# A CIN kernel on one core: first transfers, first gathers and first products in another order

## Chip, cores and metric

The kernel runs on one core of a Trainium2 chip. The metric is the device time of one execution, in microseconds (us). Before the change the median of 7 runs is 767.29 us, from 765.71 to 769.38.

## What is computed

Three layers of a compressed interaction network on `x` of shape (1024, 39, 64), then a linear layer. Cut to what matters:

```python
def _cin_layer(Xk, X0, W, b):
    Wr = W.reshape(O, Hk, Fdim)
    return jnp.einsum('bhe,bfe,ohf->boe', Xk, X0, Wr) + b[None, :, None]
X0 = sparse_embedding; Xk = X0; outs = []
for W, b in ((W0, b0), (W1, b1), (W2, b2)):
    Xk = _cin_layer(Xk, X0, W, b)
    outs.append(Xk.sum(axis=-1))
y = jnp.concatenate(outs, axis=-1) @ fc_w.T + fc_b
```

Nothing but sums follows the second and third layer, so the kernel folds their weights with `fc_w` ahead of the main loop. What is left per batch block are products of pairs of fields, `x[i] * x[k]`, and one matrix multiplication of each with 128 output rows (64 of layer 1, 64 of the folded rest).

## The kernel before, in words

**Blocks and steps.** The batch is cut into 32 blocks of 2048 columns (32 samples by 64). A block needs six "pairs" of tiles (128 x 2048 each), and two neighbouring blocks share one "half" step of 64 + 64 rows: 208 steps in all. In each, VectorE multiplies two SBUF tiles into `p` (line 377, or 379 for the half step `u * v`), and TensorE multiplies `p` with the 128 x 128 weights `wa[:, c]` into PSUM (line 391). The head of the list is `(0,0) (0,1) (0,3) (1,0) (1,1) (1,3) (0,2) (0,4) (0,5) (0,6) (1,2) (1,4) (1,5)`: block, then pair; pair 6 is the half step. I call them step 0 to step 12 and their products p0 to p12. Pairs 0 to 5 take the tiles (0,1), (0,2), (0,3), (1,2), (2,3), (1,3) of the block. There are four `p` buffers, so product k waits for the matmuls of step k-4.

**Tiles.** The four tiles of a block, and `u` and `v`, are gathered row by row from a table in DRAM, `xd` (line 122, indirect DMAs that GpSimd issues, 1 MB each). I write r00 for tile 0 of block 0, r13 for tile 3 of block 1. `xd` is filled from `x` by `load` (line 115; blocks 0 and 1 on GpSimd's queue, later ones on SyncE's) and a row of ones (line 188). The gathers' index lists are worked out by some 45 tiny VectorE operations.

**Weights.** The folded weights go through a DRAM table too. `w2` (lines 182, 190) times `fc` gives V2 (matmuls `pv`, line 278, four transposes, line 289, copies, lines 293 and 294); V2 times `w1` gives `pt` and `pr` (lines 322 and 331); these and `w0` make `part` and `rest`, which three DMAs write into `table` (lines 342 to 344). From there two gathers per pair c, `wa` and `wb` (line 351), fetch the rows of both orders of the fields, and VectorE adds them (line 471, `add(c)`). I write wa0, wb0 for pair 0.

**What sets the order.** All of it is written by hand. Each engine works its own list in the order of the program text. GpSimd's list in the head is: load 0, load 1, r00, r01, r02, r10, r11, then, when `table` has landed, wa0 wb0 wa1 wb1 wa3 wb3 r12 wa2 wb2 r03 wa4 wb4 wa5 wb5 u v wa6 wb6 r13, and then the tiles of block 2. VectorE's list behind p4 is p5 p6 p7 add2 p8 add4 p9 add5 p10 add6 p11. The framework gives each transfer one of eight semaphores in turn, eight for the queues of SyncE and ScalarE together and eight for GpSimd's: the ninth transfer is issued only when the first has landed. So ScalarE's issue of `w0s` (line 196) waits for three earlier transfers, and ScalarE's copies of `fc` (lines 199, 200), which `pv` needs, stand behind it in ScalarE's list. `spin(n)` is n matmuls on zeros that keep TensorE busy while it waits (lines 209 to 211).

## Time and profile before

| what | value |
|---|---|
| profiled execution, device time | 766.58 us |
| its span of instructions | 764.8 us, so 1.8 us lie around it |
| TensorE busy in the span | 743.5 us (97%) |
| VectorE / ScalarE / GpSimd busy | 641.2 (84%) / 160.2 (21%) / 318.8 us (42%) |
| bytes moved by DMA | 181.79 MB, mean 238 GB/s |
| matmuls of the main loop (line 391), 1792 records | 722.5 us busy |

A row of the timeline is: start in us, duration in us, engine, line, operation, output<-input, and in brackets the engine's idle time ahead of it with what ended it. In the chain of waits a row is: start, duration, what. A TensorE step of 128 rows is 4 matmuls of 512 columns in 32-bit floats, which the trace records as 8 passes. A GpSimd row of an indirect DMA is the time in which GpSimd issues it, not the time in which the bytes move.

### The profile page before, as it was taken

The page shows a single profiled execution, that of the slowest core. Times are in us where ns is not written, and L with a number is a line of the kernel's source. Part 1 is how long each engine was busy: PE and PEld are TensorE (multiplying, and loading weights), DVE is VectorE, ACT ScalarE, POOL GpSimd, SP SyncE. Part 2 cuts the span into 40 slices and gives each one's busy share as a digit, 9 for nine tenths or more (in the row PEclk, how much of TensorE's full clock was granted, in tenths as well). Part 3 has the DMA queues.
Part 4 walks back from the last instruction along what each step waited for, and adds up shares of the span by engine and source line. Part 5 has one row for each costly group of instructions (what it writes and reads, how often), then busy time and mean ns, then how long its engine had stood idle before and what let it go on. Part 6 is the DMA issues. An engine that isn't in the chain of part 4 may idle for free.

```text
span 764.8 us, 5146 instructions
## 1 busy us (share of the span) xinstructions
PE 743.5 (97%) x1856; PEld 321.7 (42%) x1856; DVE 641.2 (84%) x479; ACT 160.2 (21%) x207; POOL 318.8 (42%) x185
## 2 busy tenths in 40 slices
PE   6598999999999999999999999999999999999998
PEld 1243444444444444444444444444444444444443
DVE  5375998899888888988888988888988888998885
ACT  2002311112221212222121222112122221112212
POOL 4387173532436354243624425363442636334200
PEclk9899999999999999999999999999999999999999
DMA  8849968575875757686565777657577764738400
GB/s 251 274 169 370 404 192 340 194 270 204 330 250 218 277 171 270 231 327 241 206 279 170 279 248 301 250 186 287 183 288 253 273 263 145 284 150 314 165 0 0
DMA packets 62839, 181.79 MB, mean 238 GB/s; under 512 B 41364, under 2 KB 41499, under 8 KB 42254
## 3 DMA queue, kind: packets, MB, share of 16 engines
q0 software_dynamic: 23712, 169.34, 57.7%
q1 hardware_dynamic: 38494, 11.36, 6.3%
q10 hardware_dynamic: 608, 0.77, 0.4%
q8 instruction: 14, 0.23, 0.1%
q14 instruction: 11, 0.09, 0.0%
HBM read 180.58 MB, written 11.10 MB: 251 GB/s over the span
## 4 chain that ended last, share of the span: by engine, by line
PE 91%; DMA 4%; issue 2%; POOL 1%; DVE 0%; ACT 0%; SPq 0%; DVEq 0%; POOLq 0%
PE po L391 91%; DMA table<-part 1%; DMA wb<-table,wlists 1%; DMA u<-xd,lists 1%; POOL wa L351 1%; DMA b0s<-in_b 1%; POOL wb L351 1%; DMA fc<-in_fc_w 1%; PE pv L278 0%; DMA xd<-in_x 0%; PE pt L322 0%; PE idle L211 0%; POOL r L122 0%; DVE g L430 0%; DVE part L337 0%
## 5 line engine op out<-in xcount | busy, mean ns | idle before, releaser
L391 PE MATMUL po<-p,wa 128*128 128x512 f32 (+1 forms) x1792 | 722.5, 595 | 10.7 <-DVE wa L471 10.6
L377 DVE TENSOR_TENSOR p<-r 128x2048 f32<-128x2048 f32 x192 | 434.3, 2290 | 88.4 <-PE po L391 82.0
L391 PEld LDWEIGHTS po<-p,wa 128*128 128x128 f32 (+1 forms) x1792 | 314.4, 190 | 418.1 <-issue 394.4
L122 POOL DMA_INDIRECT r<-xd,lists x128 | 248.8, 1944 | 365.3 <-DVE p L377 339.0
L410 ACT ACTIVATE x<-po,b0s 64x512 f32<-64x512 f32 x124 | 84.3, 683 | 355.0 <-PE po L391 348.4
L404 ACT COPY g<-u 39x1024 f32<-39x1024 f32 x64 | 66.6, 1043 | 214.8 <-DVE sums L421 176.2
L416 DVE SCALAR_TENSOR_TENSOR g<-po,fc,x 64x512 f32<-64x512 f32 x124 | 86.4, 734 | 0.0
L421 DVE TENSOR_REDUCE sums<-g 103x16 f32<-103x1024 f32 x62 | 75.6, 1220 | 2.1
L379 DVE TENSOR_TENSOR p<-u,v 128x2048 f32<-128x2048 f32 x16 | 36.6, 2285 | 7.6 <-DMA v<-xd,lists 7.6
L122 POOL DMA_INDIRECT u<-xd,lists x16 | 28.6, 1786 | 4.9 <-issue 4.6
L122 POOL DMA_INDIRECT v<-xd,lists x16 | 17.2, 1075 | 4.9 <-issue 4.9
L351 POOL DMA_INDIRECT wa<-table,wlists x7 | 9.3, 1330 | 15.3 <-DMA xd<-in_x 13.4
L211 PE MATMUL idle<-zeros 128*128 128x512 f32 x24 | 12.9, 686 | 1.5 <-DVE fc L171 1.5
L351 POOL DMA_INDIRECT wb<-table,wlists x7 | 10.8, 1544 | 2.1 <-issue 2.1
L471 DVE TENSOR_TENSOR wa<-wa,wb 128x128 f32<-128x128 f32 x7 | 2.1, 300 | 9.9 <-DMA wa<-table,wlists 7.9
L278 PE MATMUL pv<-w2s,fc 64*32 64x320 f32 x16 | 2.8, 765 | 5.8 <-DMA b0s<-in_b 5.8
L211 PEld LDWEIGHTS idle<-zeros 128*128 128x128 f32 x24 | 4.8, 212 | 8.2 <-issue 6.8
L430 DVE SCALAR_TENSOR_TENSOR g<-po,fc,x1q 64x512 f32<-64x512 f32 x4 | 3.0, 743 | 5.3 <-ACT x1q L429 5.3
L289 DVE STREAM_TRANSPOSE blocks<-pv 64x320 f32<-64x320 f32 x4 | 2.1, 513 | 5.0 <-PE pv L278 4.8
L429 ACT ACTIVATE x1q<-po,b0s 64x512 f32<-64x512 f32 x4 | 2.7, 684 | 10.2 <-PE po L391 10.2
L278 PEld LDWEIGHTS pv<-w2s,fc 64*32 64x32 f32 x16 | 1.0, 142 | 8.0 <-issue 7.3
L432 DVE TENSOR_REDUCE sums<-g 103x8 f32<-103x512 f32 x4 | 2.7, 686 | 0.1
(74 smaller groups left out, 30.2 us busy)
## 6 DMA issues: line engine op xcount, KB each, us to landing
xd<-in_x SPq DMA_DIRECT2D x30, 312.0 KB
r<-xd,lists POOLq DMA_INDIRECT x128
w2s<-in_w SPq DMA_DIRECT2D x2, 312.0 KB
xd<-in_x POOLq DMA_DIRECT2D x2, 312.0 KB
w1s<-in_w SPq DMA_DIRECT2D x2, 312.0 KB
table<-part SPq DMA_DIRECT2D x1, 320.0 KB
table<-part ACTq DMA_DIRECT2D x1, 320.0 KB
w0s<-in_w0t ACTq DMA_DIRECT2D x2, 156.0 KB
```

What stands on the lines that cost most here:

```text
L122: nc.gpsimd.indirect_dma_start(dst, None, table, bass.IndirectOffsetOnAxis(ap=lists[:, k : k + 1], axis=0))
L211: nc.tensor.matmul(idle, zeros[:, 0:128], zeros, start=True, stop=True)
L278: nc.tensor.matmul(pv[k][32 * u : 32 * u + 32, 0:320], fc2[rows], w2v[rows, f0 : f0 + 10, :], start=True, stop=True,)
L351: nc.gpsimd.indirect_dma_start(w[:, c], None, table[:], bass.IndirectOffsetOnAxis(ap=wlists[:, k, c : c + 1], axis=0))
L377: nc.vector.tensor_tensor(p, rt[n % 2][:, i], rt[n % 2][:, k], ALU.mult)
L379: nc.vector.tensor_tensor(p, ut[n // 2 % 2], vt[n // 2 % 2], ALU.mult)
L391: nc.tensor.matmul(po[n + h][m], wa[w, c, :], p[w, bass.ts(m, MM)], start=c == opens[n + h], stop=c == closes[n + h],)
L404: nc.scalar.copy(gt[H : H + F], ut[n // 2 % 2][h : h + F, bass.ts(m, SUB)])
L410: nc.scalar.activation(x1[m // 2][:, bass.ts(m % 2, MM)], po[n][m][H:128], AF.Identity, bias=b0s[H:128])
L416: nc.vector.scalar_tensor_tensor(gt[0:H, at], po[n][m][0:H], fc[:, 0:1], x1[m // 2][:, at], ALU.add, ALU.mult)
L421: nc.vector.tensor_reduce(sums[:, b_at : b_at + SB], gt.rearrange("p (b e) -> p b e", e=E), AX.X, ALU.add)
L430: nc.vector.scalar_tensor_tensor(gt[0:H], po[n][m][0:H], fc[:, 0:1], t, ALU.add, ALU.mult)
```

## The change

Four parts, all in the head of the program.

- **First transfers.** `w2` and `w1` are split over SyncE's and ScalarE's queues instead of SyncE's alone; `w0s` and `w0r` go from ScalarE's queue to SyncE's; the two rows of ones for table 0 go from ScalarE's queue to GpSimd's, ahead of load 1. SyncE and ScalarE together then have eight transfers ahead of the biases. The memsets of `v2` and `rest` go from GpSimd to VectorE, and the two copies of `fc` into `fc2` stand ahead of those into `v2`.
- **Gathers.** Only r00 and r01 are issued ahead of the weights' table. GpSimd's list behind it is now: wa0 wb0 r02 wa1 wb1 r10 r11 wa3 wb3 r12 wa2 wb2 r03 u v wa4 wb4 wa5 wb5 wa6 wb6 r13.
- **VectorE.** The list for u and v is worked out behind the V2 copies, the lists for the weights' gathers behind the `part` and `rest` copies. In the main loop's head the order p0 p1 add0 p2 add1 add3 p3 becomes p0 add0 p1 add1 p2 add3 p3.
- **TensorE.** `spin(9)` becomes `spin(11)`.

```diff
         nc.vector.memset(fc2, 0.0)
+        nc.vector.memset(v2, 0.0)
         nc.vector.memset(ones, 1.0)
+        nc.vector.memset(rest[:, NR], 0.0)
         load(0, nc.gpsimd)
         nc.gpsimd.memset(w0s, 0.0)
         nc.gpsimd.memset(w0r, 0.0)
-        load(1, nc.gpsimd)
-        nc.gpsimd.memset(v2, 0.0)
-        nc.gpsimd.memset(rest[:, NR], 0.0)
...
-        halves(w2s, w2)
-        halves(w1s, w1)
+        load_ones(0, nc.gpsimd)
+        load(1, nc.gpsimd)
+
         nc.scalar.dma_start(fc, fc_w.rearrange("o (l h) -> h (o l)", h=H))
-        load_ones(0, nc.scalar)
+        for dst, w in ((w2s, w2), (w1s, w1)):
+            for s, engine in enumerate((nc.sync, nc.scalar)):
+                engine.dma_start(
+                    dst[H * s : H * s + H], w[:, s * (FH // 2) : (s + 1) * (FH // 2)]
+                )
+        for k in range(2):
+            nc.sync.dma_start(w0s[H * k : H * k + F], w0t[:, NA * k : NA * (k + 1), :])
+        nc.sync.dma_start(w0r[0:F], w0t[:, 2 * NA : F, :])
         nc.scalar.copy(warm, warm)
-        for k in range(2):
-            nc.scalar.dma_start(w0s[H * k : H * k + F], w0t[:, NA * k : NA * (k + 1), :])
-        nc.scalar.dma_start(w0r[0:F], w0t[:, 2 * NA : F, :])
         for s in range(2):
             nc.scalar.copy(fc2[H * s : H * s + H, 0:1], fc[:, 2:3])
+        for s in range(2):
             nc.scalar.copy(v2[H * s : H * s + H, F:FT], fc[:, 1:2])
...
-        roll(0, (0, 1, 2))
-        roll(1, (0, 1))
+        roll(0, (0, 1))
...
-        spin(9)
+        spin(11)
...
     weights(0)
+    roll(0, (2,))
     weights(1)
+    roll(1, (0, 1))
     weights(3)
     roll(1, (2,))
     weights(2)
     roll(0, (3,))
+    roll_half(0)
     weights(4)
     weights(5)
-    roll_half(0)
     weights(6)
     roll(1, (3,))
...
-    p = {s: product(*s) for s in steps[:2]}
+    p = {steps[0]: product(*steps[0])}
...
     add(steps[0][1])
-    p[steps[2]] = product(*steps[2])
-    add(steps[1][1])
-    add(steps[2][1])
-    p[steps[3]] = product(*steps[3])
+    for k in (1, 2, 3):
+        p[steps[k]] = product(*steps[k])
+        if k < 3:
+            add(steps[k][1])
```

The two blocks of tiny VectorE operations that move are not shown; they are the same operations at another place.

## The prediction

> **What bounds the kernel now.** I read the page's busy line first (TensorE 97%), then the chain of waits in order of time, because a change in the head can only pay at the places where the chain leaves TensorE.

> ```profile
> 10.56 0.47 issue
> 11.03 2.84 PE pv L278 x15
> ...
> 18.19 8.48 DMA table<-part
> 26.67 0.02 issue
> 26.68 2.19 DMA xd<-in_x
> 28.88 0.45 issue
> 29.32 0.95 POOL wa L351
> ...
> 66.36 3.70 PE po L391 x8
> 70.06 0.03 issue
> 70.09 689.69 PE po L391 x1720
> ```

> From 70.09 on TensorE is the chain, without a break, to 759.78: nothing there can change. Step 9 starts at 70.09, and **the question is only when step 9 starts after the change**. A step is 3.43 us (TensorE's timeline: 64 passes, the eight steps 0 to 7, from 34.79 to 63.96; the last 61 run at 0.43 us each, the first few slower). Eight steps at 3.43 are 27.5 of these 29.2 us; the other 1.7 us go with a clock that had halved:

> ```profile
> 30.00:31.00 1.00, 0.00 (x0) 0.00 (x0) 0.00 (x0) 0.00 (x0) 0.69 (x2) 0.96 0.97 234
> 31.00:32.00 1.00, 0.00 (x0) 0.00 (x0) 0.00 (x0) 0.00 (x0) 0.69 (x2) 0.50 0.84 198
> 36.00:37.00 1.00, 1.00 (x2) 0.45 (x2) 0.84 (x1) 0.00 (x0) 1.00 (x1) 0.50 0.71 185
> ```

> The third column from the right is the granted clock: TensorE is idle from 26.5, drops to 0.50 about 4.5 us later and is back at 38. So before: start at 34.79 + 9 steps 30.9 + clock 1.7 + 2.7 in which TensorE waits for p9 and p10 = 70.09.

> Then I read GpSimd's and VectorE's timelines side by side, since all gathers go through GpSimd.

> ```profile
> 53.70 0.94 POOL L122 DMA_INDIRECT u<-xd,lists  x1 [0.30 <-issue]
> 54.95 1.89 POOL L122 DMA_INDIRECT v<-xd,lists  x1 [0.31 <-issue]
> 57.15 0.95 POOL L351 DMA_INDIRECT wa<-table,wlists  x1 [0.30 <-issue]
> 58.40 0.95 POOL L351 DMA_INDIRECT wb<-table,wlists  x1 [0.30 <-issue]
> 59.65 0.94 POOL L122 DMA_INDIRECT r<-xd,lists  x1 [0.30 <-issue]
> ```

> ```profile
> 53.70 2.33 DVE L377 TENSOR_TENSOR p<-r 128x2048 f32<-128x2048 f32 x1 [0.91 <-PE po L391]
> 55.95 0.28 DVE L471 TENSOR_TENSOR wa<-wa,wb 128x128 f32<-128x128 f32 x1
> 63.81 2.29 DVE L379 TENSOR_TENSOR p<-u,v 128x2048 f32<-128x2048 f32 x1 [7.58 <-DMA v<-xd,lists]
> 66.02 0.28 DVE L471 TENSOR_TENSOR wa<-wa,wb 128x128 f32<-128x128 f32 x1
> 67.54 2.29 DVE L377 TENSOR_TENSOR p<-r 128x2048 f32<-128x2048 f32 x1 [1.24 <-DMA r<-xd,lists]
> 69.75 0.28 DVE L471 TENSOR_TENSOR wa<-wa,wb 128x128 f32<-128x128 f32 x1
> ```

> Two things. First, an issue costs 0.94 us, and 1.25 with the gap behind it, but one that starts while a product runs ends 0.81 us after the product's end: v, 54.95 to 56.84, against p8's end at 56.03. Second, step 9 hangs on r13: it is issued at 59.65, lands by 67.5, then p10, then add6 (69.75), which stands behind p10 in VectorE's list, then step 9. **GpSimd's list, not the table alone, sets step 9.** From wa0 (29.32) to r13 it takes 30.3 us for 18 issues: 18 x 1.25 = 22.5, and 7.8 behind seven blocked ones.

> [...]

> **Part by part.**

> *pv.* Now it starts at 11.03, behind ScalarE's two w0 issues (9.41 to 10.75, its timeline). After the change it needs fc (landed at 4.84) and both halves of w2. Lower bound: 4.84 and two copies, 5.3. Upper bound: 11.03. The halves now share the engines with w1 and load 0. By the DMA column of the windows 0.39 MB have moved by 4.0 us, 0.86 by 6.0, 1.48 by 8.0; with 0.64 MB of w2 and some 0.25 of w1 ahead, about 6.1, and 1.2 for the landing: I take 7.3, a gain of 3.7. [...]

> *To the table.* From pv to the table's first DMA is 18.19 - 11.03 = 7.16 us of work that stays: 14.5. From there to wa0 is 11.13 us now, with three more megabytes of gathers queued ahead. After: r00 and r01 are issued at about 11 (load 0 shares with more: 9.83 + 1.2), and 2.1 MB of tiles and 0.82 MB of table move at about 0.39 MB per us (the windows from 16 to 20 us: 385 and 397 GB/s), from 13.3 to 20.8, and 2.0 for landing and pick-up: **wa0 at 22.8**. Bounds: 14.5 + 4.1 (the landing of the tiny fc) + 2 = 20.6, and 14.5 + 11.1 = 25.6.

> *Hidden edits, taken at nothing.* The two memsets (0.23 and 0.29 on GpSimd now) make VectorE's lists some 0.2 us later, under load 0's landing. The ones on GpSimd cost about 1 us each and push back load 1, which nothing needs before r10. Biases queue behind w0 on SyncE; the first reader is TensorE behind the spins. Two more spins, 2 x 0.89, end at about 24.4, ahead of add0. The u, v list (2.2 us of tiny operations) fits beside pv and pt; uncovered it would cost wa0 up to 0.5. The weights' lists run under the table's landing.

> *The walk from wa0 at 22.8.* 21 issues follow now instead of 18. Rules from the rows: 1.25 per issue, product end + 0.81 + 0.30 when blocked, product 2.29, first tile of an empty queue 5.7 us after issue (37.96 to 43.69), a weight about 2 us after its issue's end.
> - wa0 22.8, wb0, r02 25.3, wa1, wb1, r10 29.05, r11, wa3 31.55. add0 as now 4.96 behind wa0, step 0 at 28.3 (34.79 now). r02 lands at 31.0: p1 to 33.35, p2 to 35.8. These block wa3 (to 34.15) and wb3 (to 36.6).
> - r12 36.9, wa2 38.15. wb3 lands at 38.6: add3, step 2 at 39, p3 to 41.15, which blocks wb2 (to 41.95). **r03 at 42.25; now 42.86.** The lead of 6.5 us is used up here: three tiles more behind the table, and TensorE early but waiting for them.
> - r12 landed: p4 and p5 from 42.65 to 47.15 block u and v. r03 landed: p6, p7, p8, p9 follow from 47.4 to 57.25 nearly without a break and block wa4, wb4, wa5, wb5 (to 58.05). wa6 58.35, wb6 59.6, **r13 at 60.85; now 59.65.**
> - Step 8 needs add5 (wb5 landed, 60.4) and runs from 60.5 to 63.9. r13 lands 5.4 later, 66.3, without u and v ahead of it; p10 to 68.65, add6, **step 9 at 68.9**.

> Sum: 70.09 - 68.9 = 1.2 us gained; 766.58 - 1.2 = **765.4 us** on the profiled execution's scale. The median of the shown runs is 0.7 above that execution; the same step from it gives 766.1.

> **Rivals.**

> *The lead lives.* If fewer issues fall into products, r13 follows wa0 at the pace of the issues now (30.3 us / 18 = 1.68): 20 or 21 of these are 34.5, r13 at 57.3, step 9 at 65.4, a gain of 4.7, **761.9**. For it: some issues in the walk start within half a microsecond of a product (r03), and an earlier wa0 (20.6) brings 1.5 to 2 more. Against: p5 to p9 stand close in both walks.

> *Slower: r13 later than 62.0.* Then step 9 starts after 70.09. Each further issue that a product catches costs 1.0 to 1.3 us, and in the walk two (wa2, r03) pass only just; both caught, r13 is at 63.2 and step 9 at 71.3. TensorE is then idle for over 5 us ahead of step 9, longer than the 4.5 after which the clock fell above, and a halved clock costs another 1.7: **769.5**. It decides from r13 at 62.0 (or at 60.5 when the clock falls).

> *The table is not earlier.* Three queues at once may delay w2 and load 0 so that wa0 comes at 25.6; with most of the walk shifting by that (about 0.7 of it), r13 is at 62.8: step 9 at 70.9, **767.4**.

> **Numbers.** Chances: forecast 0.45, lead lives 0.32, r13 late and clock halved 0.15, table not earlier 0.08. About 0.2% (1.5 us) is what a measurement of this kernel can tell from no change. The forecast's own range is 763.5 to 767, so it gives faster 0.19, same 0.25, slower 0.01; the second gives faster 0.28, same 0.04; the third slower 0.12, same 0.03; the last slower 0.04, same 0.04. Together faster 0.47, same 0.36, slower 0.17. The range reaches to the second and third: 760.5 to 769.

> **What would show it.** Right: wa0 at 21 to 24.5, step 0 near 28, r03 near 42, issues of about 2 us from 43 to 58, r13 near 60, step 9 near 69, and a gap of some 5 us in TensorE ahead of step 9. Wrong: r13 before 58 or behind 62, a table that lands after 24, or a wait of the main stream behind step 9.

## The result and the profile after

The kernel after takes **770.21 us** (median of 19 runs, 767.65 to 772.66), the kernel before beside it 767.06 us (45 runs, 764.98 to 769.83). The ratio is 1.0037, with a 95% interval of 1.0027 to 1.0047: **slower by 0.37%**, some 3 us, where 765.4 us and a small gain were forecast. The profiled execution of after took 767.86 us (span 766.1 us).

Its chain of waits in order of time (start, duration, what), parts of it:

```profile
1.52 7.17 DMA w2s<-in_w
8.83 2.54 PE pv L264 x14
...
15.65 7.73 DMA table<-part
23.40 1.23 DMA xd<-in_x
24.62 0.49 issue
25.12 0.95 POOL wa L350
...
61.60 5.37 DMA r<-xd,lists
...
69.30 0.30 DVE wa L472
69.64 691.28 PE po L392 x1720
```

The table is written from 15.65 instead of 18.19, and wa0 is issued at 25.12 instead of 29.32: a lead of 4.2 us. Of it 0.45 us are left at step 9 (69.64 instead of 70.09). And the stream behind it, the same 1720 passes, takes 691.28 instead of 689.69 us. Windows of 1 us of after; behind the busy times of five engines stand the granted clock, the DMA share and GB/s:

```profile
68.00:69.00 1.00, 0.00 (x0) 0.00 (x0) 1.00 (x1) 0.00 (x0) 1.00 (x1) 1.00 1.00 319
...
70.00:71.00 1.00, 1.00 (x4) 0.48 (x4) 1.00 (x1) 0.00 (x0) 0.70 (x2) 0.50 1.01 418
...
73.00:74.00 1.00, 1.00 (x8) 0.47 (x6) 0.99 (x1) 0.68 (x1) 1.00 (x1) 1.00 1.04 429
```

TensorE stands idle up to step 9, and just when it starts, the clock is at 0.50 (4 passes in a us instead of 8), from 69.47 to 72.89 by the trace's record of the granted clock. That costs the 1.59 us. So in the profiled executions: 0.45 us gained in the head, 1.59 lost by the clock, 1.14 us slower at the last matmul, 1.28 in device time. Before, TensorE's wait of 2.4 us ahead of step 8 left the clock at 1.00, and step 9 followed 0.03 us behind step 8.

GpSimd's and VectorE's timelines of after show where the lead went (start, duration, engine, line, operation, output<-input, idle ahead):

```profile
46.15 2.48 POOL L122 DMA_INDIRECT v<-xd,lists  x1 [0.30 <-issue]
...
57.95 2.10 POOL L350 DMA_INDIRECT wa<-table,wlists  x1 [0.30 <-issue]
60.35 0.94 POOL L350 DMA_INDIRECT wb<-table,wlists  x1 [0.30 <-issue]
61.60 0.95 POOL L122 DMA_INDIRECT r<-xd,lists  x1 [0.30 <-issue]
```

```profile
56.94 2.28 DVE L380 TENSOR_TENSOR p<-u,v 128x2048 f32<-128x2048 f32 x1
59.14 0.28 DVE L472 TENSOR_TENSOR wa<-wa,wb 128x128 f32<-128x128 f32 x1
67.09 2.29 DVE L378 TENSOR_TENSOR p<-r 128x2048 f32<-128x2048 f32 x1 [7.66 <-DMA r<-xd,lists]
69.30 0.28 DVE L472 TENSOR_TENSOR wa<-wa,wb 128x128 f32<-128x128 f32 x1
```

r13 is issued at 61.60 (before 59.65). From wa0 to r13 GpSimd needs 36.5 us for 21 issues: 21 x 1.25 = 26.3 us, and 10.2 behind nine issues that products held up (before: 30.3 us for 18, of them 7.8 behind seven). Three more issues and two more held up use up the lead of 4.2 us and 1.95 more. That step 9 is 0.45 us earlier all the same comes from r13's landing: p10 starts 5.49 us after r13's issue, before 7.89, with u and v queued shortly ahead of it. VectorE waits for r13 alone (7.66 us). TensorE's timeline of after (x counts passes):

```profile
37.97 27.95 PE L392 MATMUL po<-p,wa 128*128 128x512 f32 x64 [0.61 <-DVE wa L472]
69.64 6.78 PE L392 MATMUL po<-p,wa 64*128 64x512 f32 x19 [3.71 <-DVE wa L472]
```

Steps 1 to 8 run without a gap from 37.97 to 65.93, and then TensorE waits for add6, in one piece of 3.7 us. (Idle times of TensorE are the profile's, in which the end of a pass is modelled.)

The medians stand 3.15 us apart and the profiled executions 1.28: the profiled one lies near the lower end of after's runs. Each run lists its mean granted clock. One halved stretch of 3.41 us in 767 lowers it by 0.0022. Of 26 further runs of this kernel on record (E0's among them) three had 0.993 (median 768.96 us), 17 had 0.991 (769.49) and six had 0.989 (771.19): executions with more of the time halved are longer on the whole, though the two longest (772.66 and 772.08) had 0.991. Where in them it fell is not recorded.

### The profile page after: what moved, and what is told of

The parts are those of the page before. It is cut to its first block, busy times and chain, and to the rows that moved or that the text cites. A ratio compares the mean times of both kernels' runs of the same rounds, so it can differ in the third digit from the quotient of the medians.

```text
span 766.1 us, 5152 instructions
## 1 busy us (share of the span) xinstructions
PE 748.0 (98%) x1860; PEld 322.9 (42%) x1860; DVE 641.1 (84%) x481; ACT 160.7 (21%) x207; POOL 321.5 (42%) x185
## 4 chain that ended last, share of the span: by engine, by line
PE 91%; DMA 4%; POOL 2%; issue 2%; DVE 0%; ACTq 0%; ACT 0%; POOLq 0%; DVEq 0%; SPq 0%
PE po L392 90%; DMA v<-xd,lists 1%; DMA table<-part 1%; DMA w2s<-in_w 1%; POOL r L122 1%; POOL wa L350 1%; DMA r<-xd,lists 1%; POOL wb L350 1%; PE pv L264 0%; PE pt L304 0%; DMA xd<-in_x 0%; PE idle L210 0%; DVE g L431 0%; ACTq L186 0%; DVE part L319 0%
## 5 line engine op out<-in xcount | busy, mean ns | idle before, releaser
L122 POOL DMA_INDIRECT r<-xd,lists x128 | 249.3, 1948 | 365.9 <-DVE p L378 328.5
L380 DVE TENSOR_TENSOR p<-u,v 128x2048 f32<-128x2048 f32 x16 | 36.5, 2283 | 0.0
L122 POOL DMA_INDIRECT u<-xd,lists x16 | 30.0, 1876 | 4.9 <-issue 4.6
L122 POOL DMA_INDIRECT v<-xd,lists x16 | 17.7, 1109 | 4.9 <-issue 4.9
L350 POOL DMA_INDIRECT wa<-table,wlists x7 | 10.9, 1550 | 13.0 <-DMA xd<-in_x 11.2
L350 POOL DMA_INDIRECT wb<-table,wlists x7 | 8.7, 1248 | 2.1 <-issue 2.1
L430 ACT ACTIVATE x1q<-po,b0s 64x512 f32<-64x512 f32 x4 | 2.7, 684 | 10.2 <-PE po L392 10.2
```

Of the source, the lines that this page charges most:

```text
L122: nc.gpsimd.indirect_dma_start(dst, None, table, bass.IndirectOffsetOnAxis(ap=lists[:, k : k + 1], axis=0))
L350: nc.gpsimd.indirect_dma_start(w[:, c], None, table[:], bass.IndirectOffsetOnAxis(ap=wlists[:, k, c : c + 1], axis=0))
L380: nc.vector.tensor_tensor(p, ut[n // 2 % 2], vt[n // 2 % 2], ALU.mult)
```

## The experiments

**Theory.** GpSimd's list up to r13, slowed by VectorE's products, sets step 9; the lead at wa0 is eaten by three more tiles in that list; the single long wait that results lets the clock fall. **Rivals:** the first transfers cost by themselves (contention), or the price is the table's landing. Every run stands beside runs of the kernel before on the same chip, and ratios are to those.

### E0: the kernel after once more

> The changed kernel once more, beside the others on one chip. Theory (GpSimd's list up to r13 sets step 9, TensorE idles ahead of it and its clock halves): r13 is issued within 1 us of 61.6, step 9 starts at 69 to 71, the clock is halved there for 3.4 to 6.8 us, and the time is 770 +- 1 us. Rival (the extra time lies in the first transfers, a late w2 and table): the same time, but wa0 and step 0 vary with it and step 9 does not wait for p10.

769.99 us beside 766.66, ratio 1.0046 (1.0031 to 1.0061). wa0 25.03, r13 61.62, step 9 69.68, its stream 691.39 us with the clock halved from 69.93 to 73.35. The picture at step 9 repeats. Ahead of it one execution differs from another: step 0 is at 31.18 here (32.07 in the first profile), and TensorE waits 1.22 us ahead of step 2.

### E1: the first transfers alone, in the kernel before

```diff
+        for dst, w in ((w2s, w2), (w1s, w1)):
+            for s, engine in enumerate((nc.sync, nc.scalar)):
...
         roll(0, (0, 1, 2))
         roll(1, (0, 1))
```

> The kernel before with the first part alone: first transfers, memsets and fc copies as after the change; gathers, products and spins as before. Theory: wa0 comes some 2 us earlier than before (27 to 28), the 18 issues up to r13 take some 30 us as before, step 9 starts near 68: 765.5 us, faster than before by 1 to 2. Rival (the first transfers are what costs): slower than before, 769 to 770 us.

766.39 us, 0.9997 (0.9987 to 1.0008): no difference, where a gain of 1 to 2 us was expected. The table is written from 15.32, 2.9 earlier than before, yet wa0 comes at 28.51 (29.32 before) and r13 at 61.09. The wait was split, 2.31 us ahead of step 8 and 0.35 ahead of step 9, and behind step 9 the stream is as long as in the kernel before, so the clock stayed:

```profile
71.78 689.69 PE po L390 x1720
```

The first transfers neither cost nor gain here, so that rival falls.

### E2: the orders of gathers and products alone

The kernel after, with before's first transfers.

```diff
+        halves(w2s, w2)
+        halves(w1s, w1)
...
         roll(0, (0, 1))
```

> The changed kernel with the first transfers, memsets and fc copies of before: only the order of gathers, lists, products and the spins are new. Theory: wa0 near 27, the 21 issues take 36 us, r13 near 63, step 9 near 71.5 and a halved clock there: 771 to 773 us, slower than the whole change. Rival (the first transfers are what costs): 766 to 767 us, no slower than before.

769.62 us, 1.0027 (1.0008 to 1.0046): slower, by somewhat less than expected. The table is written from 17.74; wa0 26.55, r13 63.69, step 9 71.75 behind an idle of 4.4 us, and the clock at half from 69.69 to 76.5, which makes the stream longer:

```profile
71.75 692.04 PE po L393 x1720
```

**The part that costs is the order of the gathers with that of the products** (and the lists and spins that go with it). The earlier transfers bring nothing on top that the runs can tell: the full change stands at 1.0037 and 1.0046. The order on VectorE alone, the later place of the lists and the two more spins had no run of their own.

### E3: add6 ahead of p10

```diff
             n, c = steps[at + AHEAD]
+            if at == 6:
+                add(steps[9][1])
             p[n, c] = product(n, c)
```

> The changed kernel with one VectorE operation moved: add6 (wa + wb of the half step) ahead of p10 instead of behind it, so that step 9 no longer waits for r13. Theory: add6 runs at about 63 to 64, step 9 follows step 8 at 65.8 without a gap and at full clock, step 10 starts near 69.5 instead of 74.9: 764.8 us, 5.4 less than the changed kernel and about 2 less than before. Rival (the first transfers are what costs, or the wait is only moved to step 10): 768 to 770 us.

765.70 us, 0.9987 (0.9974 to 1.0): 4.3 us below E0 on the same chip, and level with the kernel before as far as the interval tells. VectorE's timeline of this kernel:

```profile
64.83 0.29 DVE L472 TENSOR_TENSOR wa<-wa,wb 128x128 f32<-128x128 f32 x1 [3.76 <-DMA wb<-table,wlists]
68.46 6.70 DVE L378 TENSOR_TENSOR p<-r 128x2048 f32<-128x2048 f32 x3 [3.34 <-DMA r<-xd,lists]
```

add6 runs at 64.83, as soon as wb6 is there, and step 9, whose product p9 was long done, starts at 66.1 without a gap. What waits for r13 now is step 10 (1.00 us), and steps 14 and 17 lose 0.22 and 1.16. The clock stays at 1.00. In the kernel after, step 9 did not need r13 at all: add6 only stood behind p10 in VectorE's list.

### E4: TensorE kept busy through the gap

```diff
         add(steps[at + 2][1])
+        if at == 9:
+            for m in range(4):
+                nc.tensor.matmul(po[1][m], zeros[:, 0:128], zeros, start=False, stop=False)
         multiply(n, c, p.pop((n, c)))
```

> The changed kernel with four matmuls on zeros between step 8 and step 9, which add nothing to the sums: the wait for r13 stays, TensorE is busy through it. Theory (a part of the loss is the clock that halves in that wait): step 9 still starts at 69 to 70, the clock stays full behind it, step 10 starts near 73.5 instead of 75: 768.0 us, 1.7 to 2.5 below the changed kernel (769.99 on this chip's last comparison). Rival (the clock costs nothing, the wait is all): 770 us.

767.52 us, 1.0008 (0.9994 to 1.0022). add6 runs at 69.15 (69.30 in after), so the wait is still there, but filled with zeros. Windows of this kernel:

```profile
66.00:67.00 1.00, 1.00 (x4) 0.51 (x3) 0.06 (x1) 0.00 (x0) 0.69 (x2) 1.00 1.12 254
...
71.00:72.00 1.00, 1.00 (x8) 0.51 (x6) 1.00 (x2) 0.44 (x1) 1.00 (x1) 1.00 1.05 432
```

The clock stays at 1.00. The zeros end later than add6, so step 9 starts at 70.40 (69.64 in after), and yet the median is 2.5 us below E0's (2.9 by the two ratios, since the chips differ; an estimate from their intervals is 1.3 to 4.5). The mean clocks of the unprofiled runs agree: 0.992 to 0.996 here, 0.989 to 0.991 in E0. So the halved clock costs more in the median of runs than the 1.59 us of the one profile, by the middle of that estimate. **The clock is most of the loss:** with it kept up, no difference from the kernel before is left that these runs can tell.

### E5: five products taken off VectorE

```diff
-            p[n, c] = product(n, c)
+            p[n, c] = product(n, c, at + AHEAD in range(4, 9))
...
+        if alone:
+            nc.scalar.copy(p, rt[n % 2][:, PAIRS[c][1]])
```

p4 to p8 are left out; ScalarE copies one tile in their place.

> The changed kernel with the products p4 to p8 left out: ScalarE copies one of their two tiles instead, so VectorE does nothing large from p3 to p9 (ScalarE's copies of u move behind them). Theory (a product on VectorE holds up a GpSimd issue): the issues behind r12 take 0.94 us each, r13 is issued at 53 to 56 instead of 61.6, step 9 follows step 8 without a gap: 765 us or less. Rival (what holds GpSimd up is the transfers ahead, or its list itself): issues of about 2 us stay, r13 at 60 or later, the gap ahead of step 9 stays.

763.49 us, 0.995 (0.9934 to 0.9967). GpSimd's timeline of this kernel:

```profile
45.34 0.95 POOL L122 DMA_INDIRECT r<-xd,lists  x1 [0.30 <-issue]
46.59 0.95 POOL L122 DMA_INDIRECT u<-xd,lists  x1 [0.30 <-issue]
...
56.60 0.95 POOL L122 DMA_INDIRECT r<-xd,lists  x1 [0.30 <-issue]
```

From r03 (45.34) to r13 (56.60) there are nine issues at 1.25 us, none held up: 11.3 us instead of 19.1 in after (42.49 to 61.60). Steps 3 and on run without a gap. It is the products that hold up GpSimd.

### E6: r13 right behind r03

```diff
     roll(0, (3,))
+    roll(1, (3,))
     roll_half(0)
...
     weights(6)
-    roll(1, (3,))
```

> The changed kernel with r13 issued behind r03, ahead of u, v and the weights of pairs 4, 5 and 6; nothing else. Theory (r13's place in GpSimd's list sets step 9): r13 near 45, p10 behind add5, add6 near 65 when wb6 has landed, step 9 at about 66 without a gap and at full clock: 765 us. Rival (GpSimd's list is only as long as it is, and the wait moves to u, v or wb5): a gap of 2 us or more ahead of step 8, 768 us or more.

**765.03 us, 0.9972 (0.9957 to 0.9986): faster than the kernel before, and the best complete kernel here.** r13 is issued at 46.22. TensorE's timeline of this kernel (x counts passes):

```profile
41.70 17.43 PE L392 MATMUL po<-p,wa 128*128 128x512 f32 x40 [0.64 <-DVE wa L472]
60.81 15.69 PE L392 MATMUL po<-p,wa 128*128 128x512 f32 x43 [1.68 <-issue]
```

The long wait ahead of step 9 is gone. One of 1.7 us ahead of step 7 is in its place, for wb4 and add4, since wb4, one place later in GpSimd's list, is issued at 55.77 instead of 51.15; the clock stays at 1.00, and step 9 starts at 67.9.

### E7: both halves of w2 on SyncE's queue, w1 on ScalarE's

```diff
-        for dst, w in ((w2s, w2), (w1s, w1)):
-            for s, engine in enumerate((nc.sync, nc.scalar)):
+        for dst, w, engine in ((w2s, w2, nc.sync), (w1s, w1, nc.scalar)):
+            for s in range(2):
```

> The changed kernel with both halves of w2 on SyncE's queue and both halves of w1 on ScalarE's, behind fc. Theory: w2 lands 1.2 us earlier (pv goes through from about 7.2 instead of 8.4), the table and wa0 come some 1.2 earlier, but r13 stays within 1 us of 61 and step 9 within 1 us of 69.5: 769 to 770 us. Rival (the late w2 is what costs, and each us of it comes through): 768.6 us or less, step 9 1.2 earlier.

771.26 us, 1.0049 (1.0033 to 1.0066): worse than expected. pv goes through from 6.5 and the table is written from 13.50, yet wa0 comes at 26.36, r13 at 65.47, and ahead of step 9 TensorE idles 5.2 us; the clock is at half from 72.07 to 78.9. What the earlier V2 gave was lost in the table's landing.

### E8, E12, E13: less beside the table's landing

Loads 3 to 5 (E8), loads 2 to 5 (E12), and also the rows of ones (E13) are issued behind ScalarE's first copies of u. E8:

```diff
     load(2)
-    load(3)
...
     fields(0)
+    for k in (3, 4, 5):
+        load(k, nc.scalar)
```

> The changed kernel with the loads of blocks 3, 4 and 5 issued by ScalarE behind the first copies of u, instead of by SyncE when the table has landed. Theory for the slow start (their 256-byte packets fill the queues from 23 to 30 us and delay the first weights and r02): wa0 unchanged near 25, step 0 5.5 us behind it (near 30.5, and not more), r02 lands 5.7 behind its issue instead of 7.8, step 1 near 35 instead of 37 to 38; but r13 still at 60 to 61 and step 9 within 1 us of 69.5, so the time stays 769 to 770 us. Rival (an early start comes through): step 9 two us earlier, 767.5 us or less.

> The changed kernel with the loads of blocks 2 to 5 issued by ScalarE behind the first copies of u, so that no 256-byte packets move beside the table's writes. If they are what stretches the table's landing: wa0 at 21 to 22.5 instead of 25, step 0 near 27. If they are not: wa0 at 24.5 to 26. In both cases r13 stays near 60 to 61 (the products' hold on GpSimd) and the time within 1 us of 769.5; a time of 767 us or less would say that the early table does come through.

> As the one before, with the rows of ones for tables 1 and 2 late as well, so that nothing but the two tiles moves beside the table's writes. If wa0 still comes at 24.5 to 26, the writes themselves and the two tiles are what takes the 9 us; if it comes at 22 or earlier and the one before did not, the ones are it. Time as for the one before.

769.93 us, 1.0034 (1.0017 to 1.0051); 770.45 us, 1.004 (1.002 to 1.0059); 770.08 us, 1.0027 (1.0008 to 1.0047). wa0 at 25.27, 24.99 and 25.84: the loads and the ones are not what stretches the table's landing. Step 0 does come earlier (29.52, 29.82 and 30.18 instead of 32.07 and, in E0, 31.18), since the gathers land sooner. It brings nothing: step 2 then waits (2.2, 1.5 and 2.0 us), r13 comes at 62.96, 62.63 and 64.15, and ahead of step 9 stand 3.5, 5.3 and 5.1 us. An early start does not reach step 9.

### E9, E10: r13 ahead of wa5, and that with late loads

```diff
-    roll_half(0)
     weights(4)
+    roll_half(0)
+    roll(1, (3,))
     weights(5)
     weights(6)
-    roll(1, (3,))
```

> The changed kernel with GpSimd's list behind r03 as wa4 wb4 u v r13 wa5 wb5 wa6 wb6 (r13 early, but the weights of pair 4 ahead of u and v, as they stand ahead of step 7). Theory: r13 near 54, no gap ahead of step 7 (1.8 us with r13 right behind r03) nor ahead of step 9, step 9 at 65.8: 763.5 us. Rival (the list is only as long as it is): the wait moves to v and p9, a gap of 2 us or more ahead of step 8, 765 us or more.

> The two before it together: r13 and the weights of pair 4 early, loads 3 to 5 late. Theory: with step 9 no longer bound to r13, the earlier step 1 (near 35) comes through where nothing else waits: 761.5 to 763 us, the best so far. Rival (GpSimd's list binds again at another tile): 763.5 to 765 us, with the gap that it names ahead of steps 5 to 9.

766.91 us, 0.9992 (0.9972 to 1.0012), and 766.74 us, 0.9993 (0.9976 to 1.0011): both below the kernel after, and both short of what was expected. VectorE's timeline of E9 shows why:

```profile
62.52 2.29 DVE L380 TENSOR_TENSOR p<-u,v 128x2048 f32<-128x2048 f32 x1 [5.22 <-DMA v<-xd,lists]
65.40 0.29 DVE L472 TENSOR_TENSOR wa<-wa,wb 128x128 f32<-128x128 f32 x1 [0.59 <-DMA wb<-table,wlists]
```

The wait moves to v (p9) and to wb5 (add5, 65.40): 3.4 us ahead of step 8, and the clock falls there: the 1728 passes from 65.75 take 694.82 us, 1.70 more than 689.69 for 1720 and 3.43 for a step. In E10 TensorE waits 2.34 us ahead of step 2, 0.67 ahead of step 8 and 0.94 ahead of step 17, with the clock halved once, behind the first.

### E11: no tile ahead of the table

```diff
-        roll(0, (0, 1))
...
-    roll(0, (2,))
+    roll(0, (0, 1, 2))
```

> The changed kernel with no tile ahead of the table: r00 and r01 are issued behind wa0 and wb0. It asks why the table lands at 24.5 whenever it is issued (13.5 to 16). If its bytes wait for the tiles' bytes, wa0 comes at 20 to 21.5, 4 us earlier. If the table takes its own 9 us, wa0 stays at 24.5 to 26. Either way p0 and p1 are late (r00, r01 and r02 in a row, r02 lands near 31 or 36), and the time is 769 us or more.

769.76 us, 1.0037 (1.002 to 1.0053). The table is written from 15.12 and wa0 still comes only 9.1 us later, at 24.19. Step 0 must now wait for its tile until 39.57; from there on nothing stops, and step 9 is at 72.28 with the clock at 1.00 (it came back at 42.73). This kernel is as slow as the one after, by a late start and not by a clock that falls at step 9. Such a list with late loads as well was not tried.

### E14: E6 with late loads and ones

```diff
+    for k in range(1, NTAB):
+        load_ones(k, nc.scalar)
+    for k in (2, 3, 4, 5):
+        load(k, nc.scalar)
```

> The kernel with r13 right behind r03 (765.03 us) with loads 2 to 5 and the ones late as well. Theory: r13 no longer binds, so what the table and r02 gain comes through where no other tile waits: 762.5 to 764.5 us. Rival (issues on GpSimd are as slow as the products make them, and the next tile in the list binds): 765 us or more, with a gap ahead of step 7 or step 8 instead.

765.76 us, 0.9983 (0.9968 to 0.9998): no better than E6. Step 0 comes at 29.26, and five waits give it back: 0.56 us ahead of step 1 (for r02), and 1.94, 1.06, 0.56 and 1.20 ahead of steps 2, 7, 8 and 9. Ahead of these four VectorE waits for wb3, wb4, wb5 and wb6, one entry of GpSimd's list after the other.

## Why the prediction was wrong

- **What bounds: right.** The question was when step 9 starts, and GpSimd's list up to r13 answered it (E5, E6); behind step 9 nothing but the clock changed.
- **The sum: the step that failed.** "Sum: 70.09 - 68.9 = 1.2 us gained" counts the start of step 9 alone. The same text puts TensorE's work up to 63.9 and step 9 at 68.9, so 5 us idle, gives 4.5 us as the time after which the clock fell, and prices a halved clock at 1.7, but only in the rival: behind the forecast's own gap the clock stands at nothing. By its own rule the forecast should have been 765.4 + 1.7 = 767.1 (767.8 as a median). Measured: 767.86 and 770.21; idle 3.7 us, the clock fallen, 1.59 us in the profile and some 2.5 us in the median (E4). That 3.7 us were enough also shows that the 4.5 us, read off a single wait, were no threshold (last section).
- **pv at 7.3, the table at 14.5: too early.** Its first two passes ran at 5.45, earlier than thought, but the others waited for the half of w2 on ScalarE's queue, to 8.83: the chain has that half for 7.17 us. The table began at 15.65. It did not matter for wa0: in E7, with the table from 13.50, wa0 came at 26.36.
- **wa0 at 22.8: mis-sized, 25.12.** 1.15 us of it come from the table's later start, the rest from the landing: 9.5 us from the first DMA to wa0 instead of 8.3. It lies within the bounds named (20.6 to 25.6), near the late one, and beyond the 24.5 up to which the walk was to count as right. The 1.2 and 2.0 us that the sums of pv and wa0 add for landings are the author's estimates, and no run shows them apart: measured were 7.17 us for w2's half on ScalarE's queue and the 9.5 us to wa0, landings included.
- **Step 0 at 28.3: late, 32.07.** It waits for add0, which ran 6.5 us behind wa0 (25.12 to 31.63) instead of 4.96.
- **r02 5.7 us after its issue: mis-sized, 7.8** (27.63 to p1 at 35.42), beside weights, two more tiles and loads. That put step 1 at 37.97.
- **r03 at 42.25, "the lead is used up here": right,** 42.49. The late start did little harm, since products then held up two issues ahead of r03 (r12 and wa2) instead of the three of the walk. That two mis-sized terms met so well is in part luck. E8 and E12 show the same from the other side: an earlier step 0 does not reach r13.
- **r13 at 60.85, step 9 at 68.9: near,** 61.60 and 69.64; issues of about 2 us in between, as said.
- **Hidden edits at nothing: not contradicted.** E1, which holds the memsets, the ones and the moved issues, made no difference.
- **The rivals.** "Lead lives" fell: three more tiles and the products ate it. "r13 later than 62.0" named the mechanism that came: its second condition, 60.5 when the clock falls, was met at 61.60. The walk's own r13, 60.85, lay beyond that 60.5 already. Its 769.5 us, near the median of 770.21, is luck in part: it was worked out on the profiled execution's scale (767.86 measured) with step 9 at 71.3, and the median got there with more time lost to the clock than 1.7 us. "The table is not earlier" was half true (wa0 25.12 against 25.6).
- **Products hold up GpSimd's issues: right.** The 21 issues from wa0 to r13 took 36.5 us where 21 x 1.25 are 26.3, and in E5, without p4 to p8, no issue between r03 and r13 was held up. The issues seen held up are all indirect DMAs; how a plain DMA's issue fares beside a product no run here shows.
- **Left open.** The profiles account for 1.3 of the 3.1 us, the runs of E4 for 2.5. How often the clock stays down for longer in unprofiled runs was not seen directly.

## What to carry to other kernels

When a hand-written list is reordered, follow it to the last entry that the steady part waits for: moving one entry (E6) or one small operation that stood behind a wait it did not need (E3) was worth more than 4 us against the kernel after, while of a first gather 4.2 us earlier 0.45 us were left at step 9. Price each idle stretch of TensorE with the clock that follows it; one wait of 3.7 us (after) was followed by half clock, 2.31 and 0.35 us apart (E1) were not. A gain at the front of such a list has to be walked through all its waits, for in E8 to E10 and E14 the next entry took the place of the one that was mended.

## What the runs showed of the hardware

**An earlier write of the table did not bring an equally early first gather.** From the write to wa0 it took 11.1 us in before and 13.2 in E1, with five tiles queued ahead; 9.5 in after, 8.8 in E2 and 12.9 in E7 with two; and 9.1 in E11 without any. The latest write with two tiles ahead (17.74, E2) waited least and the earliest (13.50, E7) most. Taking the loads and ones away (E13: 10.2 us) did not shorten it, and its cause stays open.
